# A gate's Silu split into a copy at once and a Silu four slots later, in the lines layer of a four-layer scan kernel

## Chip, cores and metric

The kernel runs on one core of a Trainium2 chip, in float32 throughout. The metric is the device time of one execution in microseconds (us), lower is better. The engines are named as the profile names them: PE (TensorE), DVE (VectorE), ACT (ScalarE), POOL (GpSimd) and SP (the queue that issues the DMAs).

## The reference, cut to what matters

Eight images of 48x48 pixels with 96 channels pass four residual layers, each behind a group norm. Layers 0 and 3 are two-dimensional selective scans (`ss2d`), layer 1 is an up-sampled small network, and layer 2, the lines layer, is a selective scan along the rows and columns of the image in four directions, each with its own weights. Only layer 2 is touched. For one direction it computes:

```python
xz = x @ in_w
xi, z = jnp.split(xz, 2, axis=-1)                 # 192 channels each
xi = jax.nn.silu(causal_conv4(xi) + conv_b)
dt_low, Bm, Cm = jnp.split(xi @ xproj_w, [6, 22], axis=-1)
dt = jax.nn.softplus(dt_low @ dt_w + dt_b)
y = selective_scan(xi, dt, -jnp.exp(A_log), Bm, Cm, D)   # h = exp(dt*A)*h + dt*B*u ; y = C.h + D*u
y = y * jax.nn.silu(z)                            # the gate
return y @ outp_w
```

The results of the four directions are joined, multiplied by `out_w` and added to x. Three different functions of ACT are needed for each piece of a direction: Silu (twice: for the convolution and for the gate), Softplus, and the many Exp of the scan.

## The kernel before

**Tiling.** The lines layer works through 160 blocks: 8 images x 4 directions x 5 blocks of 480 (four of them) or 384 (one) pixels. The 192 channels lie as two halves of 96. A block's scan has 16 states x 192 channels, cut into 8 groups of three units ("slots"), and two slots make a turn: a block has 4 turns and 8 slots. A turn has three scan instructions on DVE (`scan`, L331), each over two units.

**One turn** is written out by hand in `scans`. `make_da` (L323) takes the Exp on ACT into the PSUM tile `ps_da`, of which there are two; `copy_b` (L280) copies B into the single PSUM tile `ps_b`; `make_dbu` (L299) multiplies on DVE and POOL into `dbu`; `scan` runs on DVE; `make_hc` (L337) multiplies by C on POOL; `reduce` (L353, L357, L359) sums on PE into `ps_y`; `done` (L931) multiplies `ps_y` by the gate `zb` on DVE; then `project` (L940) on PE, into bank `ps_sa`, and `add` (L946 or L948) on DVE put the result into x. Each engine takes its instructions in the order of this program text.

**The preparation of later blocks** (`stage1`) is cut into steps that hang on slots. `aside(at)` runs what is due at slot `at`, in the middle of a turn. For the block that comes next or after next, with the slot taken modulo 8:

- slots 3 and 4: `conv`, the convolution on PE (L866), into `ps_sb` and `ps_sa`;
- slot 6: `s2`, two Silus on ACT from these banks into `ub` (L875), then `s3`, the x-projection on PE (L885) into `ps_sa`;
- slot 7: `s4`, the copy of its result to `bcl` on ACT (L890), then the dt-projection on PE (L896);
- slot 0: `s6`, the store of B and C (L900, SP) and two Softplus on ACT into `dds` (L903);
- slot 1: `s7`, the gate's product with the weights on PE (L909) into `ps_sa` and `ps_sb`, dt*u on POOL (L499), and two stores of `dds` to DRAM by SP (L485);
- slot 2: `s8`, two Silus on ACT from these two banks into the SBUF tile `zb` (L918), and in the same slot `project` of the block before, which wants bank `ps_sa`.

SP loads `dd`, the broadcast of what L485 stored, in slots 3 and 5 (L252), and B and C in slots 1, 6 and 7 (L264). The steps of slots 0 to 2 belong to the block after the running one; those of slots 3 to 7 to the next but one. `zb` lives in pool `u`, with two buffers.

**The guest.** Layer 1 runs inside layer 0 and layer 2 as a guest: in slots 0, 2, 3 and 6 it may put one group of matmuls into a free bank (`ps_sa` or `ps_sb`), and its result is copied out by ACT at the start of the next slot (`settle`; L1140 to L1233, tile `g_room`).

**Tables.** Before an ACT function whose table isn't the active one the compiler puts an ACT_TABLE_LOAD. The profile shows it with the line of the instruction that it serves: L918 and L875 for a Silu, L903 for a Softplus, L323 for the Exp that follows. A copy needs none.

Of the kernel before, what the change touches and what calls it, by code (L numbers as in the profile page):

```python
# [10 lines left out]
AF = mybir.ActivationFunctionType  # L11
# [6 lines left out]
DH = 96  # L18
NS = 16
NK = 4  # L20
# [81 lines left out]
def vss_stack_kernel(ctx: ExitStack, tc: tile.TileContext, i: dict, out: bass.AP):  # L102
    nc = tc.nc
    nb = i["x"].shape[0]
# [379 lines left out]
    def store_dd(b, half):  # L484
        nc.sync.dma_start(b.dd[half].rearrange("j (g m) -> g j m", g=3), b.dds[:, half].rearrange("p t m -> p (t m)"))  # L485

    def sizes(b, half):

        return [b.dds[:, half, n, b.at] for n in range(2)]

    def make_room(b, pools):
        b.room = pools["dds"].tile([DH, LEAD + 4 * WMAX], F32, tag="dds", name="dds")
        b.dds = b.room[:, LEAD:LEAD + 4 * b.m].rearrange("p (h t m) -> p h t m", h=2, t=2)

    def make_du(b, u):


        dt, du = [b.dds[:, :, n, b.at].rearrange("p h (r s) -> p h r s", s=SEG) for n in range(2)]
        nc.gpsimd.tensor_mul(du, dt, u)  # L499
        if b.m == b.n:  # L500
            at = SEG - 1 if b.rev else 0
            nc.gpsimd.memset(dt[:, :, :, at:at + 1], FAR)
        else:

            far = b.dds[:, :, :, b.came:] if b.back else b.room[:, :4 * b.m].rearrange("p (u m) -> p u m", m=b.m)[:, :, :LEAD + 1]
            nc.gpsimd.memset(b.dds[:, :, :, 0:1] if b.back else b.dds[:, :, :, b.goes:], 0.0)
            nc.gpsimd.memset(far, FAR)
# [265 lines left out]
    def lines(xin, xout, guest):  # L773
# [22 lines left out]
        def shift(t, dy, dx):  # L796

            at = (pad + dy) * step + pad + dx
            return t[:, at:at + H * step].rearrange("p (h w) -> p h w", w=step)[:, :, :W]
# [43 lines left out]
        for k in range(NK):  # L843
            nc.vector.tensor_mul(taps[:, k], taps[:, k], wl["l2_inu"][:, k].unsqueeze(1).to_broadcast([DH, 4, 2 * DH]))
            for half in range(2):
                nc.scalar.activation(diag[:, k, half, :], wc["ident"], AF.Identity, scale=w["l2_d"][:, k, half:half + 1])

                p = ps("sa" if half else "sb", 1)
                nc.tensor.matmul(p[:DH, :C], lhsT=wl["l2_outpt"][:, k, half, :], rhs=wl["l2_out"][:, k, :],
                                 start=True, stop=True)  # L850
                nc.scalar.copy(wo[:, k, half, :], p[:DH, :C])
        def stage1(b):
            n = b.n
            col, rev = dirs[b.k]
            got = {}

            def shifted(off):
                return shift(colwise if col else rowwise, 0, off)[:, b.r0:b.r0 + b.nr, :]

            def conv(half):  # L860
                def run():
                    got["u", half] = ps("sa" if half else "sb", 1)
                    for tap in range(4):
                        off = tap - 3 if not rev else 3 - tap
                        at = ((b.k * 4 + tap) * 2 + half) * DH
                        nc.tensor.matmul(got["u", half][:, :n], lhsT=wide("cw", at),  # L866
                                         rhs=shifted(off), start=(tap == 0), stop=(tap == 3))
                return run

            def s2():  # L870
                b.uball = ubs[(len(BLKS) * (NK * b.job + b.k) + (len(BLKS) - 1 - b.blk if rev else b.blk)) % 3]
                b.uball = b.uball.rearrange("p (h n) -> p h n", h=2)
                b.ub = b.uball[:DH]
                for half in range(2):
                    nc.scalar.activation(b.ub[:, half, :n], got["u", half][:DH, :n], AF.Silu,  # L875
                                         bias=w["l2_cb"][:, b.k, half:half + 1])

            def s2s3():
                s2()
                s3()  # L880

            def s3():
                got["p"] = ps("sa", 1)
                for half in range(2):
                    nc.tensor.matmul(got["p"][:, :n], lhsT=wide("xp", (2 * b.k + half) * NBC), rhs=b.uball[:, half, :n],  # L885
                                     start=(half == 0), stop=(half == 1))

            def s4():
                b.bcl = pools["bcl"]
                nc.scalar.copy(b.bcl[:NBC, :n], got["p"][:NBC, :n])  # L890

            def s5():
                s4()
                for half in range(2):
                    got[half] = ps("sb" if half else "sa", 1)
                    nc.tensor.matmul(got[half][:, :n], lhsT=wide("dtw", (2 * b.k + half) * DH), rhs=b.bcl[:, :n],  # L896
                                     start=True, stop=True)

            def s6():
                nc.sync.dma_start(b.bcd, b.bcl[:2 * NS, :n])  # L900
                make_room(b, pools)
                for half in range(2):
                    nc.scalar.activation(sizes(b, half)[0], got[half][:DH, :n], AF.Softplus,  # L903
                                         bias=w["l2_dtb"][:, b.k, half:half + 1])

            def s7():
                for half in range(2):
                    got["z", half] = ps("sb" if half else "sa", 1)
                    nc.tensor.matmul(got["z", half][:, :n], lhsT=wide("inz", (2 * b.k + half) * DH),  # L909
                                     rhs=shifted(0), start=True, stop=True)  # L910
                make_du(b, b.ub[:, :, :n].rearrange("p h (r s) -> p h r s", s=SEG))
                for half in range(2):
                    store_dd(b, half)

            def s8():
                b.zb = up.tile([DH, 2, BMAX], F32, tag="zb", name="zb")
                for half in range(2):
                    nc.scalar.activation(b.zb[:, half, :n], got["z", half][:DH, :n], AF.Silu)  # L918

            return {3: conv(0), 4: conv(1), 6: s2s3, 7: s5, 8: s6, 9: s7, 10: s8}  # L920

        def opening(b, half):
            return wide("diag", (2 * b.k + half) * DH), b.uball[:, half, :b.n]
# [57 lines left out]
        guest.psum = lambda tag: ps(tag, 1)  # L981
        guest.rate = 0.42
        scans(dirs, range(NK), True, ON_POOL_L2, a, pools, ps, stage1, opening, done, side, tail, guest=guest)
        stack.close()

# [265 lines left out]
    guest = Guest(stack, x1, x2)  # L1251
    ss2d("l0", i["x"], x1, guest)
    lines(x2, x3, guest)
    stack.close()
    ss2d("l3", x3, out)
# [94 lines left out]
```

## Time and profile before

| | |
|---|---|
| median of 3 runs (lowest, highest) | 17466.22 us (17460.61, 17471.88) |
| the profiled execution's own time | 17467.17 us |
| its span, first to last instruction | 17465.4 us |
| granted TensorE clock, mean | 0.839 |
| busy over the span: DVE, POOL, ACT, PE | 91%, 87%, 80%, 76% |
| lines layer, first to last scan | 5970 to 11900 us |
| busy in it (5930 us): DVE, POOL, ACT, PE | 5422.7, 4908.8, 4893.5, 4515.0 us |
| ACT_TABLE_LOADs: by L918, L903, L875, L323 | 160, 160, 159, 993 |

The 993 loads of L323 come from all three scan layers. Between the first and the last scan a block takes 5930 / 160 = 37.1 us. Where a view gives a sum over the stretch from 6000 to 11700 us, divide by 154 for the mean of a block (5700 / 37.1).

### The profile page before, as it was taken

The page shows a single profiled execution, that of the slowest core. Times are in us where ns is not written, and L with a number is a line of the kernel's source. Part 1 is how long each engine was busy: PE and PEld are TensorE (multiplying, and loading weights), DVE is VectorE, ACT ScalarE, POOL GpSimd, SP SyncE. Part 2 cuts the span into 40 slices and gives each one's busy share as a digit, 9 for nine tenths or more (in the row PEclk, how much of TensorE's full clock was granted, in tenths as well). Part 3 has the DMA queues.
Part 4 walks back from the last instruction along what each step waited for, and adds up shares of the span by engine and source line. Part 5 has one row for each costly group of instructions (what it writes and reads, how often), then busy time and mean ns, then how long its engine had stood idle before and what let it go on. Part 6 is the DMA issues. An engine that isn't in the chain of part 4 may idle for free.

```text
span 17465.4 us, 168933 instructions
## 1 busy us (share of the span) xinstructions
PE 13240.6 (76%) x53740; PEld 4749.1 (27%) x53740; DVE 15969.0 (91%) x9976; ACT 13903.6 (80%) x20972; POOL 15179.8 (87%) x8015
## 2 busy tenths in 40 slices
PE   6778787878787677777777777776777777777776
PEld 1223232333232333233233322222222222222221
DVE  7999999999999799899889999996999999999998
ACT  6878878878787688888788888886878878878776
POOL 7988888988888788888788888886999999999998
PEclk7878888888897888899889888887878878878877
DMA  4554555454555444444444444443555555455454
GB/s 139 179 169 167 174 166 175 169 177 168 165 176 172 135 147 162 147 158 156 153 154 155 153 155 156 153 157 125 173 174 171 176 168 178 171 170 177 169 177 145
DMA packets 887918, 2843.65 MB, mean 163 GB/s; under 512 B 353468, under 2 KB 421788, under 8 KB 760206
## 3 DMA queue, kind: packets, MB, share of 16 engines
q1 hardware_dynamic: 887022, 2832.85, 47.7%
q8 instruction: 422, 6.91, 0.2%
q14 instruction: 474, 3.88, 0.1%
HBM read 2384.40 MB, written 448.17 MB: 162 GB/s over the span
## 4 chain that ended last, share of the span: by engine, by line
DVE 22%; ACT 21%; POOL 19%; issue 14%; PE 13%; DMA 10%; SPq 1%; POOLq 0%; DVEq 0%; ACTq 0%
DVE dbu L331 14%; POOL dbu L337 12%; ACT ps_da L323 7%; DVE dbu L299 6%; POOL dbu L299 5%; DMA dd<-dds 4%; DMA dd<-dd 3%; ACT L323 3%; PE ps_y L357 2%; POOL dds L499 2%; ACT ps_b L280 1%; PE ps_sa L940 1%; PE ps_sa L885 1%; DMA bc<-bcd 1%; ACT L903 1%
## 5 line engine op out<-in xcount | busy, mean ns | idle before, releaser
L331 DVE TENSOR_TENSOR_SCAN dbu<-ps_da,dbu 128x968 f32<-128x968 f32 (+3 forms) x5760 | 11825.2, 2075 | 770.4 <-ACT ps_da L323 610.2
L337 POOL TENSOR_TENSOR dbu<-dbu,bc 128x1440 f32<-128x1440 f32 (+1 forms) x3840 | 10064.7, 2633 | 1941.7 <-DVE dbu L331 1860.2
L323 ACT ACTIVATE ps_da<-dd,w_l_a 128x484 f32<-128x484 f32 (+3 forms) x11520 | 7426.2, 649 | 2436.5 <-DVE dbu L331 2202.9
L357 PE MATMUL ps_y<-dbu,w_red 128*32 128x480 f32 (+1 forms) x23040 | 4253.3, 658 | 1600.6 <-POOL dbu L337 1572.4
L359 PE MATMUL ps_y<-dbu,w_red 128*32 128x480 f32 (+1 forms) x7680 | 4215.2, 657 | 0.0
L299 DVE TENSOR_TENSOR dbu<-dd,ps_b 128x962 f32<-128x962 f32 (+5 forms) x2880 | 3831.5, 1330 | 265.6 <-ACT ps_b L280 156.1
L299 POOL TENSOR_TENSOR dbu<-dd,bc 128x481 f32<-128x481 f32 (+5 forms) x2240 | 3911.2, 1761 | 23.6 <-DMA dd<-dd 19.0
L357 PEld LDWEIGHTS ps_y<-dbu,w_red 128*32 128x32 f32 x23040 | 729.0, 118 | 5033.5 <-POOL dbu L337 3369.4
L280 ACT COPY ps_b<-bc 128x482 f32<-128x482 f32 (+3 forms) x2720 | 1449.2, 533 | 214.7 <-DVE dbu L299 167.3
L574 PE MATMUL ps_side<-xpad,w_l_cw 128*128 128x480 f32 (+1 forms) x2880 | 1342.0, 604 | 48.4 <-ACT g_room L1176 16.9
L323 ACT ACT_TABLE_LOAD x993 | 1274.0, 1283 | 17.8
L703 PE MATMUL ps_s<-bcl,square 128*128 128x480 f32 (+1 forms) x1280 | 888.0, 785 | 323.2 <-ACT dds L707 163.8
L353 PE MATMUL ps_y<-big,eye 128*128 128x480 f32 (+1 forms) x960 | 748.3, 868 | 231.8 <-ACT big L754 227.4
L713 PE MATMUL ps_s<-big,square 128*128 128x480 f32 (+1 forms) x1280 | 849.4, 794 | 65.4 <-ACT g_room L1176 18.5
L499 POOL TENSOR_TENSOR dds<-dds,big 96x960 f32<-96x960 f32 (+1 forms) x320 | 705.9, 2206 | 166.6 <-ACT dds L731 166.2
L574 PEld LDWEIGHTS ps_side<-xpad,w_l_cw 128*128 128x128 f32 x2880 | 570.4, 209 | 804.9 <-issue 696.6
L885 PE MATMUL ps_sa<-ub,square 128*128 128x480 f32 (+1 forms) x640 | 405.0, 770 | 382.9 <-ACT ub L875 382.9
L359 PEld LDWEIGHTS ps_y<-dbu,w_red 128*32 128x32 f32 x7680 | 666.7, 118 | 0.0
L866 PE MATMUL ps_sb<-xpad,square 128*128 128x480 f32 (+1 forms) x1280 | 600.5, 615 | 85.0 <-ACT g_room L1176 31.3
L866 PE MATMUL ps_sa<-xpad,square 128*128 128x480 f32 (+1 forms) x1280 | 538.0, 561 | 0.0
L707 ACT ACTIVATE dds<-ps_s,w_l_dtb 96x480 f32<-96x480 f32 (+1 forms) x640 | 405.1, 633 | 123.4 <-DMA dd<-dds 71.0
L754 ACT COPY big<-ps_y 96x480 f32<-96x480 f32 (+1 forms) x640 | 471.0, 736 | 34.7 <-PE ps_y L359 33.3
(243 smaller groups left out, 12648.2 us busy)
## 6 DMA issues: line engine op xcount, KB each, us to landing
dd<-dd SPq DMA_DIRECT2D x512, 1452.0 KB
bc<-bcd SPq DMA_DIRECT2D x1536, 480.0 KB
dd<-dd SPq DMA_DIRECT2D x256, 1440.0 KB
dd<-dds SPq DMA_DIRECT2D x512, 363.0 KB
dd<-dd SPq DMA_DIRECT2D x128, 1164.0 KB
bc<-bcd SPq DMA_DIRECT2D x384, 384.0 KB
dd<-dds SPq DMA_DIRECT2D x256, 360.0 KB
dd<-dd SPq DMA_DIRECT2D x64, 1152.0 KB
```

Of the source, the lines that this page charges most:

```text
L280: nc.scalar.copy(bps[t][:, :bcs[t][0].shape[1]], bcs[t][0])
L299: engine.tensor_mul(o, du, by.unsqueeze(1).to_broadcast([P, hi - lo, by.shape[1]]))
L323: nc.scalar.activation(da[:, at:at + b.m], b.got[half][:, u % 3, 0, :], AF.Exp, scale=a[:, b.k, ci:ci + 1])
L331: nc.vector.tensor_tensor_scan(db, da, db, 0.0, ALU.mult, ALU.add)
L337: nc.gpsimd.tensor_mul(h, h, bcs.pop(2 * t + sub)[1].unsqueeze(1).to_broadcast([P, 3, n]))
L357: nc.tensor.matmul(y[32 * g:32 * g + 32, :n], lhsT=wc["red"][:, :32], rhs=hc[:, g, b.at], start=False, stop=(slot == 3))
L359: nc.tensor.matmul(y[DH:, :n], lhsT=wc["red"][:, 32:], rhs=hc[:, 2, b.at], start=False, stop=(slot == 3))
L499: nc.gpsimd.tensor_mul(du, dt, u)
L574: nc.tensor.matmul(pu[:, :n], lhsT=flat[:, at:at + P], rhs=xpad[:, r0 + dy:r0 + dy + nr, dx:dx + W], start=(tap == 0), stop=(tap == 8))
L703: nc.tensor.matmul(got["p"][:, :n], lhsT=wide("dtw", (2 * b.k + half) * DH), rhs=b.bcl[:, :n], start=True, stop=True)
L713: nc.tensor.matmul(got["p"][:, :n], lhsT=wide("xp", (2 * b.k + half) * NBC), rhs=uall[:, half], start=(half == 0), stop=(half == 1))
L866: nc.tensor.matmul(got["u", half][:, :n], lhsT=wide("cw", at), rhs=shifted(off), start=(tap == 0), stop=(tap == 3))
```

## The change

`s8` copies the two products into `zb` without a function. A closure `gate` takes the Silu of both halves in place, as one instruction of 96 x 960 (or 96 x 768), and is called at the end of `s2` of the block that comes after, four slots later, directly behind its two convolution Silus. For the last block of the layer, which has no follower, it runs by itself in the slot where that would have been. Nothing else is changed: no bank, no buffer, no DMA, no other engine's instruction.

```diff
+        raw = []
+
+        def gate():
+            while raw:
+                z = raw.pop()
+                nc.scalar.activation(z, z, AF.Silu)
+
         def stage1(b):
...
                 for half in range(2):
                     nc.scalar.activation(b.ub[:, half, :n], got["u", half][:DH, :n], AF.Silu,
                                          bias=w["l2_cb"][:, b.k, half:half + 1])
+                gate()
...
             def s8():
                 b.zb = up.tile([DH, 2, BMAX], F32, tag="zb", name="zb")
                 for half in range(2):
-                    nc.scalar.activation(b.zb[:, half, :n], got["z", half][:DH, :n], AF.Silu)
-
-            return {3: conv(0), 4: conv(1), 6: s2s3, 7: s5, 8: s6, 9: s7, 10: s8}
+                    nc.scalar.copy(b.zb[:, half, :n], got["z", half][:DH, :n])
+                raw.append(b.zb[:, :, :n])
+
+            return {3: conv(0), 4: conv(1), 6: s2s3, 7: s5, 8: s6, 9: s7, 10: s8,
+                    **({14: gate} if b.last and b.k == NK - 1 and b.job == nb - 1 else {})}
```

## The prediction

> **What bounds the kernel now.** I read the page first, then the waits between 6000 and 11700 us (the lines layer, 154 blocks of 37.1 us), then the timelines of ACT, DVE and PE around one block. On the page ACT's table loads stand high among the groups (busy time, mean ns of one, idle before):
>
> ```profile
> L323 ACT ACT_TABLE_LOAD x993 | 1274.0, 1283 | 17.8
> ```
>
> Still, DVE is the busiest engine of the layer (5422.7 of 5930 us), and ACT has 6.5 us of idle time in each block ((5930 - 4893.5) / 160). So what the loads cost is decided by what DVE waits for:
>
> ```profile
> DVE dbu L331 <- ACT ps_da L323: 248.2, 235, 2.7
> DVE x L948 <- PE ps_sa L940: 112.0, 94, 2.4
> DVE x L946 <- PE ps_sa L940: 46.5, 35, 2.5
> DVE dbu L299 <- DMA dd<-dd: 42.2, 40, 3.5
> PE ps_sa L940 <- ACT zb L918: 80.8, 73, 4.3
> ```
>
> Per block (divided by 154): 1.61 us for an Exp, 1.03 us for the out-projection before the add, 0.27 us for the broadcast dd. The last line says that PE stands still for 0.52 us before that projection because the gate's Silu holds bank ps_sa; that is in 73 of 154 blocks only.
>
> The timeline of ACT through one block (start, us, instructions, idle before in brackets), from slot 6 to slot 2:
>
> ```profile
> 8058.58 0.56 ACT L280 COPY ps_b<-bc 128x480 f32<-128x480 f32 x1 [1.20 <-DVE dbu L299]
> 8059.16 1.28 ACT L875 ACT_TABLE_LOAD   x1
> 8060.45 0.66 ACT L875 ACTIVATE ub<-ps_sb,w_l_cb 96x480 f32<-96x480 f32 x1
> 8061.01 0.65 ACT L875 ACTIVATE ub<-ps_sa,w_l_cb 96x480 f32<-96x480 f32 x1
> 8061.68 1.28 ACT L323 ACT_TABLE_LOAD   x1
> 8062.97 1.36 ACT L323 ACTIVATE ps_da<-dd,w_l_a 128x480 f32<-128x480 f32 x2
> ...
> 8072.61 1.36 ACT L323 ACTIVATE ps_da<-dd,w_l_a 128x480 f32<-128x480 f32 x2
> ...
> 8077.57 1.28 ACT L918 ACT_TABLE_LOAD   x1
> 8078.86 0.57 ACT L918 ACTIVATE zb<-ps_sa 96x480 f32<-96x480 f32 x1
> 8079.33 0.56 ACT L918 ACTIVATE zb<-ps_sb 96x480 f32<-96x480 f32 x1
> 8079.91 1.28 ACT L323 ACT_TABLE_LOAD   x1
> ```
>
> DVE at the ends of these stretches, and PE's projection:
>
> ```profile
> 8064.37 2.16 DVE L331 TENSOR_TENSOR_SCAN dbu<-ps_da,dbu 128x960 f32<-128x960 f32 x1 [0.94 <-ACT ps_da L323]
> ...
> 8074.00 2.16 DVE L331 TENSOR_TENSOR_SCAN dbu<-ps_da,dbu 128x960 f32<-128x960 f32 x1 [0.81 <-ACT ps_da L323]
> ...
> 8082.12 0.85 DVE L948 TENSOR_TENSOR x<-x,ps_sa 96x384 f32<-96x384 f32 x1 [0.31 <-PE ps_sa L940]
> ```
>
> ```profile
> 8080.53 1.56 PE L940 MATMUL ps_sa<-gated,square 96*128 96x384 f32 x4
> ```
>
> The reader is to see a lock: DVE's multiplication frees ps_b, ACT copies, loads, takes two Silus, loads, takes the Exp (ends 8064.33), and the block's first scan starts 0.04 us later. From 8058.58 to the Exp before the second stalled scan (8072.61) ACT has no idle of note. Subtracting record from record in blocks 4 to 155: the first scan starts within 0.1 us of its Exp's end in 95% of blocks, and the fourth scan (behind the Softplus) in 94%. **Slots 6 to 1 are ACT's own path; slot 2 is not.**
>
> **The Trainium skill.** "ScalarE: Activation LUTs", section "What ACT_TABLE_LOAD costs", gives about 1283 ns for the load and 1380 ns of drain, 2.66 us a switch. The trace agrees with the 1283 and shows no drain: the Silu of 8078.86 starts 0.01 us behind its load. I use 1.30 us, load and gaps. Its section "Table sets: the hidden batching unit" says that a copy is in every set; the trace agrees, L280's copies between Exps bring no load. "ScalarE activation tables: per-element evaluation and per-set limits", section "What a function is on this engine", says that the same operands cost the same whichever table is read; L890's copy takes 0.556 us beside 0.567 and 0.557 of the gate's Silus.
>
> **The change, part by part.**
>
> *Slot 2, removed:* the load before L918 and the Exp's reload behind it, 2 x 1.30 = 2.60 us of ACT per block; the copies cost what the Silus did. Over some 159 blocks ACT loses 413 us of work. Most of it is hidden: behind slot 2 ACT waits for DVE anyway (606.4 us of such waits, 3.9 us per block), and so its lead is gone well before slot 6. What is left is bank ps_sa, free 1.30 us earlier. In each block I take the smallest of PE's idle before L940, the add's own wait, and 1.3: 0.26 us in the mean, not 1.03, since in half of the blocks PE comes to L940 straight from `reduce`. The sixth slot's first Exp adds at most 0.06 us (its scan's wait).
>
> *Slot 6, added:* one Silu of 96x960 (96x768 in one block of five). The nearest rows are L731 and L610, 1.006 and 1.00 us for 96x960 and 0.84 for 96x768. Behind the Silu before it, it overlaps by 0.1 us (two Silus start 0.56 apart and take 0.66), and it has no bias operand: 0.83 us in the mean; 1.0 without the overlap is the upper end. It waits for nothing, its copy is four slots old. Queued behind it on ACT: the Exp's reload, the first Exp, L280, a guest's evacuation, bcl, Softplus. PE's x-projection needs only the Silus in front of it; PE's dt-projection and SP's store of B and C wait for bcl and move with it, and have us to spare (bc cost ACT 6.1 us in 154 blocks). No DMA is added or moved past another. DVE's next use of zb is over 20 us later.
>
> I follow the 0.83 through a block by the slack of each step:
> - first scan: +0.81 (no slack);
> - before bcl ACT waits in some blocks for PE (a guest's matmuls, the x-projection); these waits swallow 0.34, which leaves 0.49 on ACT;
> - second scan: +0.68, because 29% of the second scans waited for ACT and gain that back;
> - fourth scan, bound by ACT again: +0.44;
> - add: from +0.44 down to +0.04. Here I choose the middle: if PE's queue ahead of L940 comes later with ACT, +0.17, if not at all, -0.07;
> - seventh scan: -0.01. **On DVE alone the change is a wash.**
> - dd: POOL's dt*u (L499) stands behind L337 of the first two scans, so store and broadcast come with the second scan, +0.68, while DVE wants dd at -0.01. Dd lands 0.88 us before DVE wants it in the mean, but with a wide spread (quartiles -0.3, 0.65, 1.95), and the wait of 0.29 becomes 0.58: +0.29.
>
> Sum: -0.01 + 0.30 = +0.29 us per block, between 0.24 and 0.34 by the choice at the add; x 159 = +46 us. From the profiled execution's own time, 17467 + 46 = 17513 us; that execution lies 1 us above the median of the runs, so no correction. Unknown ends: without the overlap the gate costs 0.12 more per block (+19 us); if dd doesn't move, -0.30 (-48 us, no change in time). Other layers hold none of this.
>
> **Rivals.**
> - *Slower, the forecast:* 17513, likely 17480 to 17560.
> - *Faster:* the bank decides. PE's queue ahead of L940 runs early too, the add's wait (1.03) and the seventh scan's (0.06) go whole: 0.44 - 1.09 = -0.65; dd keeps its time and takes back 0.25: -0.40 x 159 = -63 us, 17404. For it: PE waits for zb in 73 blocks. Against: the other half. It decides from where the add gains more than about 0.75. Its far end is the plain sum of ACT, -2.60 + 0.83 = -1.77 x 159 = -281 us, 17186; 6.5 us of idle ACT speak against that.
> - *A wash:* the bank gains a little more or dd moves a little less, 17467 within 35.
> - *Much slower:* nothing swallows the delay. The fourth scan comes at +0.81 and, with the add as before and dd's further wait, I estimate +0.7 x 159 = +111, 17578. It decides if PE's waits in front of bcl move along.
> - *The change doesn't do what it says* (a load of its own for the gate, another at slot 2): no copy in the trace has one; 2 in 100, counted with the much slower.
>
> **How the numbers follow.** Forecast 0.52, faster 0.25, wash 0.13, much slower 0.10. A measurement of this kernel can tell about 0.2% (35 us) from no change. A fifth of the forecast's range lies under 35: slower 0.52 x 0.8 + 0.10 = 0.52; faster 0.25 and a little of the wash, 0.27; the rest, 0.21, the same. The range reaches to both neighbours, 17390 to 17600; the likeliest case's own is 17480 to 17560.
>
> **What would show it.** Loads of L918 gone and those of L323 down by about 160; ACT's busy time down by some 265 us (413 - 160 x 0.93, by busy time). The waits of DVE for Exp up from 1.61 us per block towards 2, nearly all at the first scan; the add's wait down by about a quarter to a half us; PE's wait for zb near nothing; DVE's wait for dd doubled. If the wait for dd doesn't grow, the loop through POOL and the DMAs is not what I take it for; if the add's wait vanishes, the faster rival is right.

## The result and the profile after

The changed kernel takes 17543.23 us in the median of 6 runs (17529.61 to 17547.56), the kernel before in the same comparison 17468.53 us (6 runs). The ratio is 1.0042 with a 95% interval of 1.0029 to 1.0055: slower by 75 us. The forecast was 17513 in a range of 17390 to 17600, most likely slower. The profiled execution takes 17529.61 us, its span 17527.8 us: 62.4 us above that of before.

The table loads went as forecast. The profile of the changed kernel has

```profile
L323 ACT ACT_TABLE_LOAD x835 | 1071.3, 1283 | 14.7
```

That is 158 loads fewer than the 993 of before at the Exp, and the 160 of the gate's own line are gone but one, at the layer's end. ACT is busy for 13631.8 us instead of 13903.6, 272 us less. And the kernel is slower.

In the waits between 6000 and 11700 us (152 blocks of 37.4 us here; name, us in total, times, longest) the lines that answer to those of before are:

```profile
DVE dbu L331 <- ACT ps_da L323: 352.2, 328, 2.7
DVE dbu L299 <- DMA dd<-dd: 88.6, 64, 4.0
DVE x L958 <- PE ps_sa L950: 50.1, 60, 2.4
DVE x L956 <- PE ps_sa L950: 24.2, 21, 2.7
PE ps_sa L950 <- ACT zb L926: 17.4, 14, 2.9
```

The projection and the add have moved to L950, L956 and L958, the gate's copy to L926. Per block DVE's wait for an Exp went from 1.61 to 2.32 us, its wait for dd from 0.27 to 0.58, its wait for the projection from 1.03 to 0.49. The bank comes free earlier (PE's wait for zb, 0.52, is 0.11 now), and what that gives is taken back twice: by the later Exp and by dd.

The timeline of ACT in slots 6 and 2 of one block (start, us, idle before in brackets):

```profile
8112.58 0.56 ACT L280 COPY ps_b<-bc 128x480 f32<-128x480 f32 x1 [1.09 <-DVE dbu L299]
8113.16 1.28 ACT L882 ACT_TABLE_LOAD   x1
8114.46 0.66 ACT L882 ACTIVATE ub<-ps_sb,w_l_cb 96x480 f32<-96x480 f32 x1
8115.02 0.65 ACT L882 ACTIVATE ub<-ps_sa,w_l_cb 96x480 f32<-96x480 f32 x1
8115.56 0.99 ACT L857 ACTIVATE zb<-zb 96x960 f32<-96x960 f32 x1
8116.57 1.28 ACT L323 ACT_TABLE_LOAD   x1
8117.87 1.36 ACT L323 ACTIVATE ps_da<-dd,w_l_a 128x480 f32<-128x480 f32 x2
...
8133.85 0.55 ACT L926 COPY zb<-ps_sa 96x480 f32<-96x480 f32 x1
8134.30 0.55 ACT L926 COPY zb<-ps_sb 96x480 f32<-96x480 f32 x1
8136.16 1.36 ACT L323 ACTIVATE ps_da<-dd,w_l_a 128x480 f32<-128x480 f32 x2 [1.31 <-DVE dbu L331]
```

and of DVE, at the block's first scan:

```profile
8119.26 2.16 DVE L331 TENSOR_TENSOR_SCAN dbu<-ps_da,dbu 128x960 f32<-128x960 f32 x1 [1.04 <-ACT ps_da L323]
```

In slot 6 the new Silu lies in the one chain that the first scan waits for: copy, load, three Silus, load, Exp (ends 8119.23), scan 0.03 us later. In slot 2 the copies run into idle time: ACT then waits 1.31 us for DVE. Over the whole layer most of the 2.6 us saved per block has become waiting. The longest of ACT's waits, in the kernel before and in the changed one, are

```profile
ACT ps_da L323 <- DVE dbu L331: 606.4, 615, 6.7
ACT ps_da L323 <- DVE dbu L331: 815.4, 813, 5.2
```

which is 3.9 and 5.4 us per block.

The distance from each scan to the next, subtracted record from record and averaged over blocks 4 to 155, shows the same account (us):

| from scan to scan | before | changed | difference |
|---|---|---|---|
| 1 to 4 | 10.21 | 10.05 | -0.16 |
| 4 to 6 | 5.56 | 5.56 | 0 |
| 6 to 7 (the add lies here) | 3.96 | 3.26 | -0.70 |
| 7 to 10 | 7.72 | 7.67 | -0.05 |
| 10 to 11 (the first use of dd) | 3.80 | 4.21 | +0.41 |
| 11 to 12 | 3.52 | 3.52 | 0 |
| 12 to the next block's 1 (slot 6's chain) | 2.32 | 3.17 | +0.85 |
| block | 37.09 | 37.43 | +0.34 |

(The rows are rounded one by one.) 0.34 x 160 = 54 us of the 62 by which the two profiled executions differ; the other 8 us lie outside the lines layer, and no run here explains them. The profiled execution of the changed kernel is also the shortest of its six, which is why 62 stands here and 75 in the medians.

### The profile page after: what moved, and what is told of

The parts are those of the page before. It is cut to its first block, busy times and chain, and to the rows that moved or that the text cites. A ratio compares the mean times of both kernels' runs of the same rounds, so it can differ in the third digit from the quotient of the medians.

```text
span 17527.8 us, 168777 instructions
## 1 busy us (share of the span) xinstructions
PE 13240.5 (76%) x53740; PEld 4737.9 (27%) x53740; DVE 15960.7 (91%) x9976; ACT 13631.8 (78%) x20816; POOL 15185.1 (87%) x8015
## 4 chain that ended last, share of the span: by engine, by line
DVE 21%; POOL 21%; ACT 19%; issue 15%; PE 12%; DMA 11%; SPq 1%; POOLq 0%; DVEq 0%; ACTq 0%
DVE dbu L331 13%; POOL dbu L337 13%; ACT ps_da L323 7%; DVE dbu L299 6%; POOL dbu L299 5%; DMA dd<-dd 4%; DMA dd<-dds 4%; ACT L323 3%; POOL dds L499 2%; PE ps_y L357 2%; ACT ps_b L280 1%; ACT L882 1%; PE ps_side L574 1%; PE ps_s L703 1%; ACT L911 1%
## 5 line engine op out<-in xcount | busy, mean ns | idle before, releaser
L893 PE MATMUL ps_sa<-ub,square 128*128 128x480 f32 (+1 forms) x640 | 443.9, 836 | 396.7 <-ACT ub L882 396.6
L873 PE MATMUL ps_sb<-xpad,square 128*128 128x480 f32 (+1 forms) x1280 | 562.0, 582 | 73.7 <-ACT g_room L1186 27.2
```

## The experiments

Each ratio is to the kernel before in the same set of runs, with a 95% interval. There were three sets, with medians of the kernel before of 17474.92 us (the halves, `gate_first`, `late_before`), 17474.86 us (the two `still` and the two `early` kernels) and 17477.26 us (the two without stores and the two with Tanh).

### Each half of the change alone

`copy_only` is the changed kernel without the gate's Silu:

```diff
                     nc.scalar.copy(b.zb[:, half, :n], got["z", half][:DH, :n])
-                raw.append(b.zb[:, :, :n])
```

> The changed kernel without the gate's Silu at slot 6: the products are only copied in slot 2, and y is multiplied by z itself. It does slot 2's half of the change alone. Theory of the slacks (slots 6 to 1 are ACT's own path, slot 2 is not): DVE gains what lay between its sixth and seventh scan, 0.45 us per block as I predicted or 0.69 as the changed kernel's trace now shows (3.96 to 3.27 us); dd keeps its time and DVE comes to it earlier, which takes back 0.16 to 0.27. Net -0.29 to -0.42 us per block, x 159 = -46 to -67 us, ratio to before 0.9962 to 0.9974. Rival, ACT's sum decides: -2.60 x 159 = -413 us, ratio 0.976. Rival, the loads of slot 2 were hidden: 1.000.

Measured: 17444.63 us, ratio 0.9984 (0.9977 to 0.9990), 30 us faster.

`both_silus` is the changed kernel with the two Silus of slot 2 put back:

```diff
-                    nc.scalar.copy(b.zb[:, half, :n], got["z", half][:DH, :n])
+                    nc.scalar.activation(b.zb[:, half, :n], got["z", half][:DH, :n], AF.Silu)
```

> The changed kernel with the Silus and their two loads left in slot 2 as before, and the in-place Silu at slot 6 besides (the gate's Silu is taken twice). It does slot 6's half alone. Theory of the slacks: the first scan +0.83, the fourth +0.44, dd with the second scan +0.68, so +0.44 on DVE and about +0.1 more by dd: +0.53 us per block, +84 us, ratio 1.0048, more than the change itself (1.0042). Rival, every us of ACT counts: +0.87 x 159 = +138 us, 1.008. Rival, the time was lost by the new order of bank ps_sa in slot 2 and not by the Silu in slot 6: 1.000.

Measured: 17571.02 us, ratio 1.0056 (1.0042 to 1.0069), 96 us slower.

The halves nearly add up: -30 + 96 = +66, where the whole has +75. Removing some 320 table loads, about 413 us of ACT's work by the prediction's 1.30 us each, is worth 30 us; adding 160 Silus, some 140 us of it, costs 96 us. That refutes the rival in which ACT's sum decides (0.976), the one in which the loads of slot 2 were wholly hidden (1.000), and for the loss the one that blames the new order of the bank in slot 2, since `both_silus` keeps the old order.

Both came out a little worse than I expected, `copy_only` outside its range. Its stretch from the sixth to the seventh scan is 3.39 us, 0.57 shorter than before, but the stretch with dd is 0.28 longer and the scans one to four 0.15 longer. The wait for dd is

```profile
DVE dbu L299 <- DMA dd<-dd: 76.9, 59, 4.9
```

where the kernel before has 42.2. That dd takes back this much is about what the theory has. The 0.15 was not in it: ACT's waits for PE ahead of bcl are 0.16 us per block longer here, and why PE comes later was not tried. In `both_silus` the first scan comes at +0.85, the fourth at +0.58 (expected: +0.83 and +0.44), and the sixth to the seventh scan shrinks by 0.20.

### Where the Silu stands in slot 6

`gate_first`:

```diff
                 b.ub = b.uball[:DH]
+                gate()
                 for half in range(2):
                     nc.scalar.activation(b.ub[:, half, :n], got["u", half][:DH, :n], AF.Silu,
                                          bias=w["l2_cb"][:, b.k, half:half + 1])
-                gate()
```

> The changed kernel with the gate's Silu ahead of the convolution's two in slot 6, instead of behind them. ACT's work is the same, the first Exp behind it is as late. But the x-projection on PE and the guest's matmuls behind it now come 0.87 later as well, so that ACT's waits for PE in front of bcl no longer swallow 0.34 us. Theory: the fourth scan 0.3 us later than in the changed kernel, +0.3 x 159 = +48 us, ratio to before about 1.007. Rival, nothing is swallowed there: same as the changed kernel, 1.0042.

Measured: 17620.3 us, ratio 1.0082 (1.0068 to 1.0096), on the side of the theory (1.007) and 0.4% above the changed kernel with the same instructions on ACT. The wait for Exp (6000 to 11700 us) is

```profile
DVE dbu L331 <- ACT ps_da L323: 444.3, 377, 2.7
```

The last two stretches before the first scan are as in the changed kernel (3.52 and 3.17 us); it is scans one to four that take 10.74 instead of 10.05 us, 0.69 more where 0.3 was expected. ACT waits for PE ahead of bcl for 1.10 us per block, 0.33 in the changed kernel and 0.55 before. So I take the x-projection and the guest's matmuls to be a second chain beside ACT's: as long as they start on time, part of the gate's Silu disappears in ACT's waits for them. The direction is shown; the size is about twice what the prediction gave to these waits, so its account of this stretch is not complete.

### The broadcast dd

`still_before` and `still_after`, the kernels before and after with

```diff
-            nc.sync.dma_start(t[:, :6 * b.m], b.dd[half].unsqueeze(1).to_broadcast([32, 4, 6 * b.m]))
+            nc.sync.dma_start(t[:, :6 * b.m], (b.dd[half] if still is None else still[half, b.n]).unsqueeze(1).to_broadcast([32, 4, 6 * b.m]))
```

where `still` holds DRAM tiles of zeros that are written once, so that the scans of these kernels work on zeros and not on dt and dt*u.

> The kernel before, but in the lines layer the broadcast dd is read from a DRAM tile that was filled with zeros once, so that it no longer waits for the store of this block's dt and dt*u (the stores stay, nobody reads them; the scans work on zeros). It takes the loop through POOL and the two DMAs away. Theory: DVE's wait for dd (0.27 us per block) goes, -0.27 x 159 = -43 us, ratio 0.9975; less, if an Exp is then what DVE waits for. Rival, dd has no part in it: 1.000.

> The changed kernel with the same zeros for dd. Theory: the wait for dd is 0.58 us per block here, twice that of before, and 0.3 us of the change's loss is the loop through POOL and the DMAs; without it the changed kernel gains 0.58 x 159 = 92 us and stands at about 0.999 of before and 0.15% above the other kernel with zeros, where it stood 0.42% above. Rival, the loss is all ACT's and dd only receives it: the distance between the two kernels with zeros stays at 0.4%.

Measured: 17455.54 us, 0.9994 (0.9984 to 1.0004), and 17515.54 us, 1.0024 (1.0016 to 1.0033). This was inconclusive. In the traces the first of a block's two broadcasts no longer waits for the store and is issued 7.5 us earlier (counted from the block's second scan; the expectation below says 5), but takes 15.7 us to land instead of 8.4, so that it lands only 0.2 us earlier. DVE's waits for it are, in the two kernels,

```profile
DVE dbu L299 <- DMA dd<-still: 28.8, 29, 4.4
DVE dbu L299 <- DMA dd<-still: 72.2, 58, 5.5
```

against 42.2 and 88.6 with the true dd. So the next two also leave the stores out:

```diff
                 make_du(b, b.ub[:, :, :n].rearrange("p h (r s) -> p h r s", s=SEG))
-                for half in range(2):
-                    store_dd(b, half)
```

> The kernel before with dd read from the tile of zeros and, besides, without the stores of dt and dt*u in the lines layer (both stay in SBUF, unread). With the stores left in, the broadcast was issued 5 us earlier but took 15.7 instead of 8.4 us and landed as late, so that run did not take the loop away; this one does. Theory: DVE's wait for dd goes to nearly nothing (0.3 us per block), about -40 us, ratio 0.998; less where an Exp is late next.

> The changed kernel in the same way. Theory: its wait for dd (0.58 us per block) goes as well, and its distance to the kernel before without stores is what ACT and the add alone make of the change: 0.15 us per block (+0.69 of waits for Exp, -0.54 at the add), about 24 us or 0.15%, instead of 0.42%. Rival, the wait for dd only takes what DVE would have waited for elsewhere: the distance stays near 0.4%.

Measured: 17383.78 us, 0.9946 (0.9934 to 0.9959), and 17398.54 us, 0.9952 (0.9940 to 0.9965). The waits of the first,

```profile
DVE dbu L331 <- ACT ps_da L323: 228.2, 230, 2.7
DVE x L948 <- PE ps_sa L940: 109.5, 90, 2.4
DVE x L946 <- PE ps_sa L940: 38.8, 34, 2.3
```

and of the second:

```profile
DVE dbu L331 <- ACT ps_da L323: 336.6, 324, 2.7
DVE x L958 <- PE ps_sa L950: 65.0, 66, 2.5
DVE x L956 <- PE ps_sa L950: 25.3, 24, 1.9
```

Neither has a wait for dd. Without the stores ahead of it the first broadcast takes 8.0 us in `nostore_before`: so it was the stores that held it up in the `still` kernels; by which way, no run shows. The same trade goes on between Exp (+108 us) and add (-58), and the stretch of slot 6 is again 0.85 us longer, but the two kernels are 15 us apart, 0.06% of the ratio, with intervals that overlap; before they were 75 apart. From the first to the last scan of the lines layer, in one profiled execution of each, the changed kernel is longer by 54.5 us as it stands, by 54.8 with zeros for dd, and by 7.2 with zeros and no stores. So **without the store that dd waits for, the change costs next to nothing; with it the gain at the add runs into dd.**

Taking the loop away gained more than its wait in the kernel before (93 us, where 0.27 us x 160 = 43): the stretch of dd lost 0.33 us, scans one to four 0.14 and scans six and seven 0.08. These two kernels leave out the stores' traffic together with the wait for them, and what each of the two adds was not separated.

### Versions that might beat both

`late_before` issues the add, and with it the guest's turn of slot 3, behind the next turn's first scan:

```diff
-            return [(1, project), (2, add)]
+            return [(1, project), (2, lambda: late.append(add))]
...
             scan(t, 0)
+            while late:
+                late.pop(0)()
```

> The kernel before, with the add (L946, L948) issued behind the next turn's first scan instead of ahead of it, and the guest's turn of slot 3 with it, which wants the same bank. If the add's wait for the projection (1.03 us per block) is on DVE's path, the seventh scan comes forward until it meets its own Exp, which has 0.95 us to spare in the mean: -0.95 us; dd takes back 0.4: -0.55 x 159 = -87 us, ratio 0.995. If that wait is only passed on to dd, 0.999 to 1.000.

Measured: 17483.06 us, ratio 1.0004 (0.9996 to 1.0013): nothing. Its waits say why:

```profile
DVE dbu L331 <- ACT ps_da L323: 402.4, 373, 2.8
DVE dbu L299 <- DMA dd<-dd: 40.0, 37, 4.8
```

The add no longer waits, and the wait for Exp is 154 us higher, as much as the add had. Both cases of my expectation are wrong on the way: it wasn't dd that took the gain. The seventh scan starts 0.9 us earlier (3.04 instead of 3.96 after the sixth) and the eighth 0.8 us later behind it (3.82 instead of 3.01). I read this as ACT, with its two loads in slot 2, being hardly ahead there; no run tries that by itself.

`early_after` and `early_before` move the step of slot 6 to slot 5 (`{..., 4: conv(1), 5: s2s3, 7: s5, ...}`; in `early_after` the last block's gate goes from step 14 to step 13).

> The changed kernel with the step of slot 6 moved to slot 5: load, two convolution Silus, the gate's Silu, reload and x-projection stand behind the turn's first Exp and no longer between the copy of B and the block's first Exp. Theory: in slot 5 the next Exp has 2.9 us to spare and ACT idles 1.9 us until the copy of B, so most of the 4.8 us is absorbed; the tenth or eleventh scan loses about 1.5 us, but the waits for Exp at scans one, two and four (2.3 us per block) shrink to under 0.5; dd takes back 0.4. Net about -0.3 to -0.8 us per block to the changed kernel, ratio to before 0.997 to 1.001. Rival, a switch of tables costs the same wherever it stands: 1.004.

> The kernel before with the same step moved to slot 5 (without a gate's Silu in it, 3.9 us). Theory: the tenth scan loses about 0.7 us, the waits for Exp at scans one, two and four (1.5 us) go; dd takes back 0.4: about -0.4 us per block, -64 us, ratio 0.996. If the Silu's place counts for nothing: 1.000.

Measured: 17589.77 us, 1.0065 (1.0052 to 1.0077), and 17531.85 us, 1.0033 (1.0021 to 1.0046). Both are wrong in sign. Of `early_before` the last stretch shrinks from 2.32 to 2.00 us and scans one to four from 10.21 to 9.59, as meant, but the tenth to the eleventh scan takes 5.24 instead of 3.80 us, of which dd is 0.2. I had added the idle time before an Exp to its slack over several scans; ACT can't use it, since it may be only two Exps ahead of DVE (two buffers `ps_da`). That reading was not tried by itself.

`tanh_gate` takes the gate without a table of its own, and `tanh_late` adds the edit of `late_before` to it (`half_` is a column of 0.5):

```diff
-                    nc.scalar.activation(b.zb[:, half, :n], got["z", half][:DH, :n], AF.Silu)
+                    nc.scalar.copy(b.zb[:, half, :n], got["z", half][:DH, :n])
+
+            def s9():
+                b.th = gp.tile([DH, 2, BMAX], F32, tag="gated", name="th")
+                nc.scalar.activation(b.th[:, :, :n], b.zb[:, :, :n], AF.Tanh, scale=0.5)
+                nc.scalar.activation(b.th[:, :, :n], b.th[:, :, :n], AF.Identity, bias=half_, scale=half_)
+
+            def s10():
+                z = b.zb[:, :, :n]
+                nc.gpsimd.tensor_mul(z, b.th[:, :, :n], z)
...
-            return {3: conv(0), 4: conv(1), 6: s2s3, 7: s5, 8: s6, 9: s7, 10: s8}
+            return {3: conv(0), 4: conv(1), 6: s2s3, 7: s5, 8: s6, 9: s7, 10: s8, 11: s9, 12: s10}
```

> A gate without a table of its own: slot 2 copies as in the change, slot 3 takes Tanh of z/2 and half of it plus a half on ACT (two instructions of 96x960, 1.9 us; in this program Tanh brings no load beside Exp), slot 4 multiplies by z on POOL (1.9 us, as L499). Slot 6 is as before. ACT saves 2.6 - 1.9 = 0.7 us in slots 2 and 3 and adds nothing where it is the path. Theory: the gain of the copy alone (-28 us measured, 0.9984) if POOL's 1.9 us find room, up to +1.9 us less what POOL idles (6 us per block) if they don't: ratio 0.998 to 1.003.

> The gate by Tanh together with the late add. With the late add alone the wait for the projection became a wait for Exp at the seventh and eighth scan (ratio 1.0004); with 0.7 us less of ACT's work in slots 2 and 3, and the loads gone from slot 2, some of that should be DVE's. Theory: 0.3 to 0.5 us per block less than the Tanh kernel, -50 to -80 us, ratio 0.995 to 0.999; if ACT's two additional instructions in slot 3 stand before the eighth scan's Exp instead, no better than it.

Measured: 17609.42 us, 1.0077 (1.0063 to 1.0091), and 17593.79 us, 1.0067 (1.0054 to 1.0079). Both lie above what was expected (at most 1.003 and 0.999). In the waits of the first,

```profile
DVE dbu L331 <- ACT ps_da L323: 367.7, 316, 3.1
DVE gated L943 <- POOL zb L930: 89.9, 78, 2.1
DVE dbu L299 <- DMA dd<-dd: 23.7, 18, 4.6
```

the gate on DVE now waits for POOL's multiplication (0.6 us per block), and the Exp behind slot 3 is late: the seventh to the eighth scan takes 3.63 instead of 3.01 us. ACT's two instructions take 0.97 and 1.16 us in the mean: the 0.5 us that ACT saves in sum stand against 2.1 us that it now has in slot 3. The first of these losses comes from my edit and not from Tanh: `th` is a tile with the tag `gated` in a pool of one buffer, so that DVE's first product of a block, which writes `gated`, has to wait until POOL has read `th`. Its own `zb` was finished a block earlier. A version with a buffer of its own for `th` was not tried, so these two runs don't say what a gate by Tanh can reach. Of the versions here that compute the whole reference, none beat the kernel before.

## Why the prediction came out right, and where it was off

- **The cost of the gate's Silu.** 0.83 us predicted; L857 takes 0.995 us for 96x960 and 0.835 for 96x768 and overlaps by 0.11, 0.85 in the mean. At the first scan +0.81 was predicted, +0.85 measured. Right. The rows named in the prediction (1.006 and 0.84 us) give 0.87 with its overlap of 0.1, so the 0.83 was a little low.
- **The slack of ACT behind slot 2.** Right in kind: `copy_only` gains 30 us for 413 us of work. The 3.9 us per block are all of ACT's waits of that kind, though; 0.7 of them lie behind the fourth scan, ahead of slot 2.
- **What ACT's waits swallow.** This step failed in size. 0.34 us were to vanish ahead of bcl and the fourth scan was to come at +0.44. The waits there fell only from 0.55 to 0.33, and the scans one to four made up 0.16 us: the fourth scan comes at +0.69, nearer to the +0.81 of the much slower rival. `gate_first` shows that the mechanism is there. In `both_silus` 0.27 are made up; `copy_only` loses 0.15 in the same scans, which the prediction put at nothing.
- **The bank.** Also off, to the other side: the sixth to the seventh scan was to gain 0.40 at the add and 0.05 at the Exp, and gained 0.70. The term that was too small is the bank's: `copy_only`, where nothing delays ACT, gains 0.57 there, for the 0.26 and at most 0.06 of the prediction. The delay alone gains 0.20 (`both_silus`). PE's wait for zb nearly went (0.52 to 0.11), and the add's own wait fell by 0.54, half of the 1.03 of the faster rival.
- **DVE alone a wash.** Predicted -0.01 us at the seventh scan; by the table it is 0.85 - 0.16 - 0.70 = -0.01. Two errors of a quarter of a us cancelled: that this number is exact is luck. `nostore_after` beside `nostore_before` is nearly the same statement measured (15 us).
- **dd.** Its wait was to go from 0.29 to 0.58 us, and went from 0.27 to 0.58; the stretch grew by 0.41. The mechanism is in the traces: in both kernels dt*u starts on POOL 4.74 us after the second scan and the first broadcast is issued 16.51 us after it, in the mean. The second scan comes at +0.76, for the +0.68 predicted, and DVE comes to dd no later than before.
- **The sum.** +46 us predicted, +62 in the profiled execution, +75 in the medians. The likely case's range, 17480 to 17560, held it. Of the 16 us between +46 and +62 half lie in the layer, where the dd stretch has +0.41 for +0.30, and half outside it.
- **Rivals.** The faster one lost at the points I named, but not by much at the first: the stretch of the add gained 0.70, short of 0.75. At the second it is clear: dd did not keep its time and took back 0.41. Both halves of the change have the sign that the theory gives them, and their sum (+66) leaves 9 us of the +75, too little for another mechanism of the size of either.

## What to carry to other kernels

A saving and a cost on the same engine don't add: price each in the slot where it stands, by what the next engine waits for. Here 2.6 us of ACT removed where it has slack bought 0.2 us per block (`copy_only`), and 0.85 us added to the chain of copy, table, Silu, table and Exp cost 0.6 (`both_silus`). When two loops through a block are nearly as long as each other (here DVE's own and store, broadcast, first use), shortening one gives the time to the other; take one of them away in an experiment and see what is left of the change. And a new temporary tile needs a buffer of its own: one that shares a buffer with another engine's output brings a wait that has nothing to do with the idea under test.

## What the runs showed of the hardware

A broadcast of 1.4 MB that was issued 7.5 us earlier, without waiting for the two stores of 0.36 MB ahead of it in its queue, landed only 0.2 us earlier: it took 15.7 us from issue to landing instead of 8.4 (`still_before` beside the kernel before). Without the stores it took 8.0 (`nostore_before`). And Tanh needed no table load beside Exp in this program (1 load for 160 Tanh in `tanh_gate`), while Silu and Softplus did (160 each at their lines, beside the reloads for Exp).
